# Two graph layers in one kernel: the second layer's loads issued by the sync engine, and its first 21 tiles gathered before the first layer's last rows are there

## The chip, the cores and the metric

One core of a Trainium2 chip runs the whole program. The metric is device microseconds of one execution; lower is better. The engines are named as the profile names them: PE is TensorE, DVE is VectorE, ACT is ScalarE, POOL is GpSimd, SP is SyncE. SP and ACT can issue plain DMA transfers; POOL issues the indirect ones, which gather or scatter 128 rows by a list of row numbers. Each engine works through its own instructions in the order in which the program lists them.

## The reference, cut to what matters

There are 6250 nodes with 256 features and 106250 edges, sorted by their destination. The last 6250 source rows belong to self loops. Both layers read one row per edge and sum over the edges that end in one node.

```python
x = _layernorm(x + L0(x, src, dst, edge_type_2))     # layer one
x = _layernorm(x + L1(x, [src, dst]))                # layer two

# L0: two relu products per edge, with the weights of the edge's type, summed by dst,
#     then gates, sigmoid, tanh and three small products per node
msgs = where(rel == r, relu(relu(S @ W.T + b) @ W.T + b), msgs)     # S = feat[src]
agg  = segment_sum(msgs, dst)

# L1: graph attention with 4 heads of 64
h     = x @ W
e     = leaky_relu(a_src[src] + a_dst[dst], 0.2)
ex    = exp(e - segment_max(e, dst)[dst])
out   = segment_sum(h[src] * ex / segment_sum(ex, dst)[dst], dst)
y     = relu(layernorm(out + x))
```

Layer two can read a node's row of `h` only after layer one has made that node.

## The kernel before

Edges other than the self loops are held as 782 tiles of 128 edges (TC). Seven tiles make a window of at most 64 destination nodes, 112 windows in all (NW), and two windows make a group of up to 128 nodes, 56 groups (NG). Self loops are handled with the node itself.

Before the layers, `gnn_kernel` reads the edge list, packs it, and turns it into lists by tile: the row numbers that layer one (`idx0`) and layer two (`idx1`) gather, each window's first node (`low_b`, a copy on every partition, and `low_i`), and the place of each edge's node in its window. In the same stretch, PE makes a table of messages, two rows a node (L1191, L1205, added up by DVE at L1213 and stored by SP at L1218); the code ties pieces of the list work to the blocks of this table, by hand.

`fast` then runs both layers under an order written out by hand: what each engine does is listed step by step, one step a tile. `Steps` holds chains of work as generators; `yield n` in a chain means "go on n steps later". `ring` hands out buffers in rotation, and a buffer's next use waits for its last reader.

Layer one: each step issues one gather on POOL (L1327) into one of ten buffers G of seven tiles each. LAG = 4 steps later PE multiplies the tile with a one-hot matrix of its nodes (`sum0`, L1689), which sums by node. After a group's last tile its rows go through `turn` and `update`: gates, products, normalization, and at L1625 the row of `h` with the logits a_src and a_dst behind it. ACT copies it into a buffer `hr` (L1629), and SP stores it into the DRAM table `rows1`, 64 rows a window (L1636). Windows overlap, so a store of 64 rows writes rows that the next store writes again. The last group's rows are scattered by POOL (L1638), since they end irregularly. Groups go through `update` in fours, then in twos, and the last four singly. The product that is kept for a node's own use later goes to the DRAM table `kept` (L1645).

Layer two: each step issues one gather of 128 rows of 260 numbers from `rows1` (L2002, through L1327) into the same ring of ten G. All of them come after all stores into `rows1`. LAG steps behind, when a window is complete, ACT copies its logits out of G (L2024; the first tile of the next group at L2016). Groups are taken in pairs, the last four singly (26 pairs and 4 groups):

- `ahead` loads what a pair needs from DRAM: the edges' places `dB` (L1764, four loads a pair) and the starts of the nodes' runs `cut` (L1771, two loads). Five steps later DVE turns dB into one-hot matrices (L1778), and PE fetches the nodes' logits with them (L1782).
- `weights` finds the largest logit of each node by scans and takes the exponential (L1822 to L1853).
- `weighted` multiplies a window's gathered rows by these weights: ACT copies the weights (L1873), DVE multiplies (L1874). This is the last reader of G.
- `sum1` sums by node on PE (L1983) and, at a group's first tile, loads `kept` rows into k3 (L1973).
- `finish` divides, normalizes twice on DVE and ACT (L1889 to L1935), and SP stores the result (L1940, two stores a group, again overlapping); POOL scatters the last group (L1942).

The loads at L1764, L1771 and L1973 are issued by ACT, in their place among ACT's copies and activations.

Of the kernel before, what the change touches and what calls it, by code (L numbers as in the profile page):

```python
# [33 lines left out]
F32 = mybir.dt.float32  # L34
I32 = mybir.dt.int32
# [39 lines left out]
NC = -(-EC // CT)  # L75
HA = D + H
LAG = 4
SORTED = "the fast path runs only where the chip has found the edges sorted"


# [623 lines left out]
def gnn_kernel(  # L704
# [37 lines left out]
    rows1 = dram.tile([NP + P, HA], F32, name="rows1")  # L742
    slots = dram.tile([NW, (WT + 1) * P], BF16, name="slots")
    cuts = dram.tile([(NC + 1) * CT, P], F32, name="cuts")
    kept = dram.tile([NG, P, 3 * D], F32, name="kept")
    packed = dram.tile([2 * BLOCKS, HB], I32, name="packed")

# [19 lines left out]
    mark = const.tile([P, COLS], BF16, name="fmark")  # L767
    tail_i = const.tile([P, 1], I32, name="tail_i")
    tail_x = const.tile([P, 1], I32, name="tail_x")


    with (
# [18 lines left out]
        with (  # L791
# [287 lines left out]
            late, turns = [], 0  # L1079
            src0 = src1  # L1080
            nc.vector.tensor_scalar(src0[:CT], src1[:CT], 1.0, None, op0=OP.subtract)
            for to, of in (
                (idx0, row),
                (dstE, list_f[:, :, 1:]),
                (mark, rel_f[:, :, :P]),
                (idx1, src0),
                (first, steps),
            ):
                for k0, kn in blocks_of(NC, 4):
                    pt = lps.tile([P, 4 * CT], F32, name="turned")  # L1090
# [15 lines left out]
                    for a, b, c in ((0, 1, 0), (1, 2, WT), (2, WT + 1, 1), (WT + 1, 2 * WT, WT + 1)):  # L1106
                        nc.vector.tensor_copy(to2[:, :, a:b], of2[:, :, c : c + b - a])
# [48 lines left out]

            nc.vector.tensor_scalar(tail_i, tail[:, 0:1], float(NP + P - 1), None, op0=OP.min)
            nc.vector.tensor_scalar(tail_x, tail[:, 0:1], float(NP - 1), None, op0=OP.min)


            for w0, wn in blocks_of(NW, P // (WT + 1)):
# [82 lines left out]
    with tc.If(odd_v == 0) as cmp:  # L1244
        fast(
            tc, x, WihT, bih, bhh, W1T, b1, W2T, b2, W3T, b3, Wg, att_src, att_dst, bias, gamma,
            beta, out, parts0, rows1, slots, cuts, kept, iota_f, iota_p, ident, idx0, idx1,
            first, mark, slot, low_i, tail_i, tail_x,
        )
    with cmp.Else():  # L1250
        general(
# [6 lines left out]
def fast(  # L1258
# [32 lines left out]
    low_i,  # L1291
    tail_i,
    tail_x,
):

    nc = tc.nc
# [27 lines left out]
        )[1]  # L1324

    def gather(to_tile, table, idx):
        nc.gpsimd.indirect_dma_start(  # L1327
            out=to_tile,
            out_offset=None,
            in_=table,  # L1330
            in_offset=bass.IndirectOffsetOnAxis(ap=idx, axis=0),
        )
# [46 lines left out]
    node3 = keep.tile([P, NG, 2, 3, 2 * H], BF16, name="node3")  # L1379
    nc.vector.memset(node3, 0.0)  # L1380
    loop = keep.tile([P, NG, H], F32, name="loop")
    vec = keep.tile([P, 2, D], F32, name="fvec")
    eps_c = keep.tile([P, 1], F32, name="eps_c")
    nc.vector.memset(eps_c, EPS)
# [32 lines left out]
    def in_order(done, g):  # L1417
        if g != len(done):
            raise ValueError("groups are out of order")
        done.append(g)  # L1420


    with (
# [32 lines left out]
        for k, v in enumerate((gamma, beta)):  # L1456
# [2 lines left out]
        nc.sync.dma_start(  # L1459
            rows1[N:, :].rearrange("(p r) f -> p (r f)", r=2),  # L1460
            zero[: (NP + P - N) // 2, : 2 * HA],
        )

        run = Steps()
# [24 lines left out]
        def turn(g, i, ps, aT):  # L1489

            agg = ring(up, [P, D], F32, "agg", 3)

            kind = ring(up, [P, 2], F32, "kind", 3)
            for r in range(2):
                nc.vector.tensor_scalar(  # L1495
                    kind[:, r : r + 1], ps[:, D:], float(3 - r), None, op0=OP.is_equal
                )
            for r, of in ((0, ps[:, :D]), (1, agg)):
                nc.vector.scalar_tensor_tensor(
                    agg,  # L1500
                    loop0[g][:, r * D : (r + 1) * D],
                    kind[:, r : r + 1],
                    of,
                    op0=OP.mult,
                    op1=OP.add,
                )
# [6 lines left out]
            nc.vector.tensor_copy(  # L1513
                aT[:, :, i * P : (i + 1) * P], pt.rearrange("p (k n) -> p k n", k=2)
            )

        def update(groups, aT):
            slow = min(3, max(1, (NG - 4 - groups[0]) // 4))
# [102 lines left out]
            for i, g in enumerate(groups):  # L1621
                u = everyone
                ph = ring(upp, [P, 4 * P], F32, "fpg", 5)[:, : D + 2 * H]
                for k in range(2):
                    nc.tensor.matmul(  # L1625
                        ph[u, :], hs[i][:, k, u], Wx[:, k, :], start=(k == 0), stop=(k == 1)
                    )
                hr = ring(up, [P, D + 2 * H], F32, "hr", 4)
                nc.scalar.copy(hr[u, :], ph[u, :])  # L1629
                nc.scalar.copy(keep3[i][u, 2, :], ph[u, :D])  # L1630

# [1 line left out]
                for w in windows_of(g):  # L1633
                    if w in at_w:
                        to = rows1[bass.ds(at_w[w], SLOTS), :]
                        nc.sync.dma_start(to, hr[half_of(w), :HA])  # L1636
                if g == NG - 1:
                    nc.gpsimd.indirect_dma_start(  # L1638
                        out=rows1,
                        out_offset=bass.IndirectOffsetOnAxis(ap=tail_i, axis=0),  # L1640
                        in_=hr[:, :HA],
                        in_offset=None,
                    )
                yield 1
                nc.sync.dma_start(kept[g, u, :], keep3[i][u, :, :].rearrange("p c f -> p (c f)"))  # L1645

# [53 lines left out]
        for n in range(TC + LAG):  # L1700
            if n < TC:
                g, t = order[n]
                k, turns = n % WT, n // WT // 10 % 2
                if k == 0:
                    seven = ring(rowsp, [P, WT * HA], F32, "G", 10).rearrange(
                        "p (j f) -> p j f", f=HA
                    )
                    m = min(WT, TC - n)
                    of, to = mark[:, n : n + m, None], seven[:, :, D : D + 1]
                    nc.scalar.copy(to[:, ::-1, :][:, :m, :] if turns else to[:, :m, :], of)  # L1710

                got[t] = seven[:, WT - 1 - k if turns else k, : D + 1]
                gather(got[t][:, :D], parts0, idx0[:, t : t + 1])
                if t == order_of(g)[0]:
                    ohs[g] = ring(ep, [P, 2 * W8, SLOTS], F32, "oh0", 2)
                    one_hot(ohs[g], 2 * g, 2 * W8)
                    loop0[g] = ring(up, [P, 2 * D], F32, "loop0", 2)
                    own_rows(g, lows_of(windows_of(g)), loop0[g], loops)
                    if g == NG - 1:
                        rows_x[g] = ring(up, [P, D], F32, "fxn", 8)  # L1720
                        own_rows(g, {}, rows_x[g], x)
            if n >= LAG:
                g, t = order[n - LAG]
                if t != 2 * WT * g:
# [4 lines left out]
                    sum0(g, 2 * WT * g)  # L1729
            run.step()  # L1730
        run.finish()


    with (
# [10 lines left out]

        nc.scalar.preload_act_table_set("natural_log_exp_and_others")
        run = Steps()
        G, late = {}, []

        def tiles_in(g):  # L1750

# [3 lines left out]
        def ahead(pair, box):  # L1755
# [5 lines left out]
            for g in pair:  # L1761
                dB = ring(ep, [P, W8, P], BF16, "dB", 3)
                for w in windows_of(g):
                    nc.scalar.dma_start(  # L1764
                        dB[half_of(w), :, :].rearrange("p j e -> p (j e)"),
                        at(slots, w * W8 * P, [[0, SLOTS], [1, W8 * P]]),
                    )
                dBs.append(dB)
            for i, g in enumerate(pair):
                n = len(tiles_in(g)[1])  # L1770
                nc.scalar.dma_start(  # L1771
                    cut[i * GS * H : (i * GS + n) * H, :],
                    at(cuts, tiles_in(g)[0][0] * P, [[P, n], [0, H], [1, P + 1]]),
                )
            yield 5
            for i, (g, dB) in enumerate(zip(pair, dBs)):
                ohT = ring(ep, [P, W8, P], BF16, "ohT", 2)
                nc.vector.tensor_scalar(ohT, dB, slot_p, None, op0=OP.is_equal)  # L1778
# [176 lines left out]
        def sum1():  # L1955
# [12 lines left out]
            if g not in sums:  # L1968
# [125 lines left out]
```

## Time and profile before

| | us |
|---|---|
| median of three runs | 2264.95 (2263.04 to 2268.02) |
| the profiled execution: its own time | 2266.64 |
| the profiled execution: span from first to last instruction | 2264.7 |
| first gather of layer one, last gather of layer one | 194.9, 1181.5 |
| first gather of layer two, last gather of layer two | 1213.8, 2198.2 |
| scatter of the last group's output | 2252.5 |

The page counts busy time by engine, and a row of an engine's timeline gives start, duration, engine, line, operation, what is written from what, and in brackets the idle time of the engine before it and what ended that. "issue" there means that no wait can be seen. ACTq, SPq and POOLq are the sequencers of these engines: a DMA's issue is not counted as busy time, but the engine does nothing else meanwhile. The granted TensorE clock has a mean of 0.81 in this execution.

### The profile page before, as it was taken

To read this page: it belongs to the slowest core of one execution; us is meant where nothing else is said; L and a number is where in the kernel's file an instruction comes from. 1 tells how busy PE (TensorE), PEld (TensorE's weight loads), DVE (VectorE), ACT (ScalarE), POOL (GpSimd) and SP (SyncE) were. 2 spreads that over 40 slices of the span, in tenths; PEclk is the share of its full clock that TensorE was granted. 3 is DMA by queue.
4 is the path that set the end of the run, shared out by engine and by line. 5 is a ranking of instruction groups with operands and counts; after the bars stand their busy time and mean duration, and the time that the engine had idled before them with its cause. 6 is when DMAs were issued, how large, how long until landed. Compare 5 with 4: busy or idle time off the path is not lost. (4 is left out here: it accounts for less than half of the span.)

```text
span 2264.7 us, 22022 instructions
## 1 busy us (share of the span) xinstructions
PE 1556.6 (69%) x5722; PEld 776.5 (34%) x5722; DVE 1237.3 (55%) x3333; ACT 508.5 (22%) x1526; POOL 1525.5 (67%) x1603
## 2 busy tenths in 40 slices
PE   8996788888888888988992355554545545454563
PEld 5663233333333333333551222222323223232331
DVE  7552133333343333433541667777776877777785
ACT  3331012222122221222342112111111111211211
POOL 1304777777777777777764777777777777777760
PEclk9998788989999989898996676766767677676776
DMA  5335445554555554555553555555555555555540
GB/s 163 131 99 157 128 128 156 168 165 143 151 155 170 165 151 143 155 170 165 176 155 91 138 161 145 154 147 155 152 149 161 144 156 151 148 156 150 156 137 27
DMA packets 163409, 332.53 MB, mean 147 GB/s; under 512 B 42467, under 2 KB 74306, under 8 KB 163273
## 3 DMA queue, kind: packets, MB, share of 16 engines
q0 software_dynamic: 75968, 208.00, 33.9%
q1 hardware_dynamic: 64736, 82.92, 11.4%
q10 hardware_dynamic: 22569, 40.12, 5.9%
q8 instruction: 47, 0.77, 0.2%
q14 instruction: 89, 0.73, 0.1%
HBM read 278.79 MB, written 52.12 MB: 146 GB/s over the span
## 5 line engine op out<-in xcount | busy, mean ns | idle before, releaser
L1327 POOL DMA_INDIRECT G<-parts,fidx x782 | 747.1, 955 | 327.5 <-issue 219.0
L1327 POOL DMA_INDIRECT G<-rows,fidx x782 | 747.5, 956 | 240.5 <-issue 222.9
L1689 PE MATMUL fps<-G,oh 128*64 128x257 f32 (+1 forms) x1674 | 533.1, 433 | 137.1 <-DMA G<-parts,fidx 120.6
L1983 PE MATMUL fps<-gw,oh 128*64 128x264 f32 (+1 forms) x1674 | 433.0, 469 | 238.3 <-DVE gw L1874 238.3
L1983 PEld LDWEIGHTS fps<-gw,oh 128*64 128x64 f32 (+1 forms) x1674 | 229.1, 168 | 412.8 <-DVE gw L1874 254.8
L1689 PEld LDWEIGHTS fps<-G,oh 128*64 128x64 f32 (+1 forms) x1674 | 196.6, 151 | 445.5 <-DMA G<-parts,fidx 226.7
L1874 DVE TENSOR_TENSOR gw<-G,bank 128x1792 f32<-128x1792 f32 (+1 forms) x167 | 249.0, 1491 | 175.0 <-ACT gw L1873 173.5
L1495 DVE TENSOR_SCALAR kind<-fps 128x1 f32<-128x1 f32 x112 | 12.5, 153 | 311.1 <-PE fps L1689 311.1
L1542 PE MATMUL fpg<-faT,fWihT 128*128 128x512 f32 (+2 forms) x432 | 171.6, 521 | 0.2 <-DVE faT L1513 0.2
L1822 PE MATMUL turn<-fident,e 128*120 128x128 f32 (+2 forms) x30 | 13.5, 449 | 219.4 <-ACT e L2016 219.4
L1410 DVE TENSOR_TENSOR oh<-bank,fslot 128x1024 f32<-128x1024 f32 x112 | 136.0, 1214 | 2.2 <-ACT bank L1853 2.2
L1923 ACT ACTIVATE frs<-fmv,eps_c 128x1 f32<-128x1 f32 x112 | 33.0, 294 | 306.0 <-DVE fmv L1922 152.0
L1650 DVE COPY nd<-hr 128x4 f32<-128x4 f32 x56 | 10.8, 193 | 160.1 <-ACT hr L1629 160.1
L1205 PE MATMUL fpm<-fWrT,fhT 128*128 128x256 f32 x392 | 91.7, 388 | 5.1 <-DVE fms L1213 5.1
L1542 PEld LDWEIGHTS fpg<-faT,fWihT 128*128 128x128 f32 x432 | 71.2, 191 | 68.9 <-issue 59.3
L1191 PE MATMUL fph<-fxc,fWrT 128*128 128x512 f32 (+1 forms) x208 | 88.9, 580 | 4.7 <-DMA fWrT<-in_WrT_dram 4.7
L1929 ACT ACTIVATE fy<-fy,frs 128x256 f32<-128x256 f32 x112 | 67.2, 600 | 98.4 <-DVE gw L1868 52.9
L1822 PEld LDWEIGHTS turn<-fident,e 128*120 128x120 f32 (+2 forms) x30 | 5.0, 166 | 233.2 <-ACT e L2016 231.6
L1205 PEld LDWEIGHTS fpm<-fWrT,fhT 128*128 128x128 f32 x392 | 74.9, 194 | 23.8 <-DVE fms L1213 8.8
L1873 ACT COPY gw<-bank 128x28 f32<-128x28 f32 (+1 forms) x167 | 28.5, 171 | 227.6 <-DMA dB<-slots 103.6
L1625 PE MATMUL fpg<-Wx,fyT 128*128 128x264 f32 x224 | 77.0, 474 | 3.0 <-ACT fyT L1616 3.0
L937 POOL DMA_INDIRECT packed<-frame,place x21 | 20.9, 995 | 77.6 <-DVE frame L902 71.5
(237 smaller groups left out, 1791.3 us busy)
## 6 DMA issues: line engine op xcount, KB each, us to landing
kept<-keep SPq DMA_DIRECT2D x56, 384.0 KB
k<-kept ACTq DMA_DIRECT2D x56, 384.0 KB
dB<-slots ACTq DMA_DIRECT2D x112, 128.0 KB
loop<-parts SPq DMA_DIRECT2D x110, 128.0 KB
parts<-fms SPq DMA_DIRECT2D x49, 256.0 KB
G<-parts,fidx POOLq DMA_INDIRECT x782
G<-rows,fidx POOLq DMA_INDIRECT x782
rows<-hr SPq DMA_DIRECT2D x110, 65.0 KB
```

The costliest lines, as they stand in the source:

```text
L1191: nc.tensor.matmul(ph[:, :cols], WrT_s[:, r, k, m * P : (m + 1) * P], xc[:, k, :cols], start=(k == 0), stop=(k == 1),)
L1205: made = nc.tensor.matmul(pm[:, r, :], hT[:, r, k, j * P : (j + 1) * P], WrT_s[:, r, k, :], start=(k == 0), stop=(k == 1),)
L1327: nc.gpsimd.indirect_dma_start(out=to_tile, out_offset=None, in_=table, in_offset=bass.IndirectOffsetOnAxis(ap=idx, axis=0),)
L1410: nc.vector.tensor_tensor(to[:, :nj, :], iota_s[:, None, :].to_broadcast([P, nj, SLOTS]), of[:, :, None].to_broadcast([P, nj, SLOTS]), op= ...
L1542: nc.tensor.matmul(pg[:, :cols], WihT_s[:, k, c * P : (c + 1) * P], aT[:, k, :cols], start=(k == 0), stop=(k == 1),)
L1625: nc.tensor.matmul(ph[u, :], hs[i][:, k, u], Wx[:, k, :], start=(k == 0), stop=(k == 1))
L1689: nc.tensor.matmul(sums[g][to, :], ohj, got[t], start=begins, stop=ends)
L1873: nc.scalar.copy(gw[:, :, D:HA], ex[:, o : o + n, :])
L1874: nc.vector.tensor_mul(gw[:, :, :D].rearrange("p j (h f) -> p j h f", h=H), of[:, :n, :D].rearrange("p j (h f) -> p j h f", h=H), ex[:, o ...
L1923: nc.scalar.activation(r, mv[u, k, 1:2], AF.Ln, bias=eps_c[u])
L1929: nc.scalar.activation(y, y, AF.Identity, bias=m, scale=r)
L1983: nc.tensor.matmul(sums[g][to, :], ohj, gw, start=begins, stop=ends)
```

## The change

Three things change.

1. The loads at L1764, L1771 and L1973 are issued by SP instead of ACT, and the reading of dB follows eight steps after them instead of five.
2. The first 21 tiles of layer two (EARLY, three windows) are gathered before layer one is done. 18 of these gathers are listed right behind layer one's last gather. They wait only for the rows of group 52 (NG - LATE - 1), by a wait that is added by hand, while the waits for the three later groups (LATE) are taken off. Three more gathers are listed behind the scatter of group 55, with a memset of one number in front. For them the row numbers `idx_e` name a row of zeros (NOROW) where the node belongs to one of the last three groups; they are made in the list stretch with some small DVE operations, as is `own_n`, the node number of each row of these three groups. The rows of `rows1` that those groups write are filled with zeros first, by one more transfer on SP.
3. What these tiles lack is added: the last three groups' rows stay in SBUF (`rows_l`, in place of a buffer `hr`, of which there are three instead of four). The edges' source numbers of the 21 tiles go to DRAM (`srcs`) and are read back on all partitions (three loads on ACT). For each of the three windows DVE compares them with `own_n`, three times 896 numbers, which gives one-hot matrices; for each tile PE multiplies three of these with `rows_l`, and DVE adds the product to the tile in G (`complete`).

```diff
+            behind.append((NB - 4, nc.sync.dma_start(srcs, src0[:EARLY, 0, :])))
...
+            for half, first_w, next_w in ((lo, w0, w0 + 1), (hi, w0 + 1, w0 + 2)):
...
+            before = lp.tile([P, EARLY], F32, name="before")
+            nc.vector.tensor_scalar(
+                before, idx1[:, :EARLY], low_b[:, w0 : w0 + 1], None, op0=OP.is_lt
+            )
...
+            nc.vector.tensor_scalar(idx_e, early_f, float(NOROW), None, op0=OP.add)
...
+        nc.sync.dma_start(
+            rows1[for_late:N, :].rearrange("(p r) f -> p (r f)", r=4),
+            zero[: (N - for_late) // 4, : 4 * HA],
+        )
...
+        def gather_early(n):
+            for t in range(len(early), n):
+                w = t // WT
+                if t % WT == 0:
+                    G[w] = ring(rowsp, [P, WT * HA], F32, "G", 10).rearrange(
+                        "p (j f) -> p j f", f=HA
+                    )
+                e = gather(G[w][:, t - WT * w, :], rows1, idx_e[:, t : t + 1])
+                for store in rest:
+                    tc.declare_no_dep(e.ins, store.ins, reason="rows of other nodes")
+                for store in whole:
+                    tc.add_manual_dep(
...
-                hr = ring(up, [P, D + 2 * H], F32, "hr", 4)
+                hr = ring(up, [P, D + 2 * H], F32, "hr", 3)
+                if g >= NG - LATE:
+                    hr = rows_l[:, g - (NG - LATE), :]
...
+            if n == TC:
+                gather_early(EARLY - 3)
...
+        nc.gpsimd.memset(pause, 0.0)
+        gather_early(EARLY)
...
+            nc.scalar.dma_start(srcb[w], at(srcs, w * WT * P, [[0, P], [1, WT * P]]))
+
+        def complete(t):
...
+                for q in range(LATE):
+                    nc.vector.tensor_scalar(
+                        srcb[w][1][:, q, :], srcb[w][0], own_n[:, q : q + 1], None, op0=OP.is_equal
+                    )
...
+            for q in range(LATE):
+                nc.tensor.matmul(
+                    more,
+                    srcb[w][1][:, q, j * P : (j + 1) * P],
+                    rows_l[:, q, :HA],
+                    start=(q == 0),
+                    stop=(q == LATE - 1),
+                )
+            nc.vector.tensor_add(G[w][:, j, :], G[w][:, j, :], more)
...
-                    nc.scalar.dma_start(
+                    nc.sync.dma_start(
                         dB[half_of(w), :, :].rearrange("p j e -> p (j e)"),
...
-                nc.scalar.dma_start(
+                nc.sync.dma_start(
                     cut[i * GS * H : (i * GS + n) * H, :],
...
-            yield 5
+            yield 8
...
-                nc.scalar.dma_start(k3s[g][u, :, :].rearrange("p c f -> p (c f)"), kept[g, u, :])
+                nc.sync.dma_start(k3s[g][u, :, :].rearrange("p c f -> p (c f)"), kept[g, u, :])
...
-            if t < TC:
+            if EARLY <= t < TC:
...
+                if k < EARLY:
+                    complete(k)
```

More of the change, by code (lines that the diff above doesn't have):

```diff
@@ L77 @@
 LAG = 4
+EARLY = 3 * WT
+LATE = 3
+NOROW = NP + SLOTS - 1
 SORTED = "the fast path runs only where the chip has found the edges sorted"
@@ L744, in gnn_kernel @@
     cuts = dram.tile([(NC + 1) * CT, P], F32, name="cuts")
+    srcs = dram.tile([EARLY, P], F32, name="srcs")
     kept = dram.tile([NG, P, 3 * D], F32, name="kept")
@@ L769, in gnn_kernel @@
     tail_x = const.tile([P, 1], I32, name="tail_x")
+    idx_e = const.tile([P, EARLY], I32, name="idx_e")
+    own_n = const.tile([P, LATE], F32, name="own_n")
     with (
@@ L1158, in gnn_kernel @@
             nc.vector.tensor_scalar(tail_x, tail[:, 0:1], float(NP - 1), None, op0=OP.min)
+            w0 = NW - 2 * LATE
+            held = lp.tile([P, LATE], F32, name="held")
+            for half, first_w, next_w in ((lo, w0, w0 + 1), (hi, w0 + 1, w0 + 2)):
+                o, v = own_n[half], held[half]
+                nc.vector.tensor_scalar(
+                    o,
+                    low_b[half, first_w : first_w + 2 * LATE - 1 : 2],
+                    iota_p[half],
+                    float(half.start or 0),
+                    op0=OP.add,
+                    op1=OP.subtract,
+                )
+                nc.vector.tensor_tensor(
+                    v, o, low_b[half, next_w : next_w + 2 * LATE - 1 : 2], op=OP.is_lt
+                )
+                nc.vector.scalar_tensor_tensor(o, o, 1.0, v, op0=OP.add, op1=OP.mult)
+                nc.vector.tensor_scalar(o, o, 1.0, None, op0=OP.subtract)
+            before = lp.tile([P, EARLY], F32, name="before")
+            nc.vector.tensor_scalar(
+                before, idx1[:, :EARLY], low_b[:, w0 : w0 + 1], None, op0=OP.is_lt
+            )
+            early_f = lp.tile([P, EARLY], F32, name="early_f")
+            nc.vector.scalar_tensor_tensor(
+                early_f, idx1[:, :EARLY], float(-NOROW), before, op0=OP.add, op1=OP.mult
+            )
+            nc.vector.tensor_scalar(idx_e, early_f, float(NOROW), None, op0=OP.add)
             for w0, wn in blocks_of(NW, P // (WT + 1)):
@@ L1247, in gnn_kernel @@
             beta, out, parts0, rows1, slots, cuts, kept, iota_f, iota_p, ident, idx0, idx1,
-            first, mark, slot, low_i, tail_i, tail_x,
+            first, mark, slot, low_i, tail_i, tail_x, idx_e, own_n, srcs,
         )
@@ L1293, in fast @@
     tail_x,
+    idx_e,
+    own_n,
+    srcs,
 ):
@@ L1326, in gather @@
     def gather(to_tile, table, idx):
-        nc.gpsimd.indirect_dma_start(
+        return nc.gpsimd.indirect_dma_start(
             out=to_tile,
@@ L1381, in fast @@
     loop = keep.tile([P, NG, H], F32, name="loop")
+    rows_l = keep.tile([P, LATE, D + 2 * H], F32, name="rows_l")
     vec = keep.tile([P, 2, D], F32, name="fvec")
@@ L1420, in in_order @@
         done.append(g)
+    G = {}
     with (
@@ L1461, in fast @@
             zero[: (NP + P - N) // 2, : 2 * HA],
+        )
+        for_late = N - 2 * LATE * SLOTS
+        nc.sync.dma_start(
+            rows1[for_late:N, :].rearrange("(p r) f -> p (r f)", r=4),
+            zero[: (N - for_late) // 4, : 4 * HA],
         )
@@ L1515, in turn, with keep_row @@
             )
+        whole, rest, early = [], [], []
+        pause = keep.tile([P, 1], F32, name="pause")
+        def keep_row(g, store):
+            if g == NG - LATE - 1:
+                whole.append(store)
+            if g >= NG - LATE:
+                rest.append(store)
+                last = store.ins.engine == mybir.EngineType.Pool
+                for e in early[: len(early) - last]:
+                    tc.declare_no_dep(store.ins, e.ins, reason="rows of other nodes")
+        def gather_early(n):
[4 more added lines that the diff above has]
+                        "p (j f) -> p j f", f=HA
+                    )
+                e = gather(G[w][:, t - WT * w, :], rows1, idx_e[:, t : t + 1])
[3 more added lines that the diff above has]
+                    tc.add_manual_dep(
+                        e.ins,
+                        store.ins.name,
+                        mybir.DependencyInfo(
+                            mybir.DependencyClass.Sync, mybir.DependencyReason.DATA
+                        ),
+                        reason="the rows that were stored by then",
+                    )
+                early.append(e)
         def update(groups, aT):
@@ L1627, in update @@
                     )
-                hr = ring(up, [P, D + 2 * H], F32, "hr", 4)
+                hr = ring(up, [P, D + 2 * H], F32, "hr", 3)
+                if g >= NG - LATE:
+                    hr = rows_l[:, g - (NG - LATE), :]
                 nc.scalar.copy(hr[u, :], ph[u, :])
@@ L1635, in update @@
                         to = rows1[bass.ds(at_w[w], SLOTS), :]
-                        nc.sync.dma_start(to, hr[half_of(w), :HA])
+                        keep_row(g, nc.sync.dma_start(to, hr[half_of(w), :HA]))
                 if g == NG - 1:
-                    nc.gpsimd.indirect_dma_start(
+                    move = nc.gpsimd.indirect_dma_start(
                         out=rows1,
@@ L1643, in update @@
                     )
+                    keep_row(g, move)
                 yield 1
@@ L1747, in fast @@
         run = Steps()
-        G, late = {}, []
+        late = []
+        srcb = []
+        for w in range(EARLY // WT):
+            srcb.append(ring(ep, [P, WT * P], F32, "srcb", 3))
+            nc.scalar.dma_start(srcb[w], at(srcs, w * WT * P, [[0, P], [1, WT * P]]))
+        def complete(t):
+            w, j = t // WT, t % WT
+            if j == 0:
+                srcb[w] = (srcb[w], ring(ep, [P, LATE, WT * P], F32, "ohS", 1))
+                for q in range(LATE):
+                    nc.vector.tensor_scalar(
+                        srcb[w][1][:, q, :], srcb[w][0], own_n[:, q : q + 1], None, op0=OP.is_equal
+                    )
+            more = ring(eps, [P, D + 2 * H], F32, "fps1", 2)[:, :HA]
+            for q in range(LATE):
[5 more added lines that the diff above has]
+                    stop=(q == LATE - 1),
+                )
+            nc.vector.tensor_add(G[w][:, j, :], G[w][:, j, :], more)
         def tiles_in(g):
```

## The prediction

> **What bounds the kernel now.** I read the page first, then GpSimd's timeline round the change of layers and at the end, the waits inside layer two, and one steady pair of groups on ScalarE and VectorE. Busy time by engine on the page:
>
> ```profile
> PE 1556.6 (69%) x5722; PEld 776.5 (34%) x5722; DVE 1237.3 (55%) x3333; ACT 508.5 (22%) x1526; POOL 1525.5 (67%) x1603
> ```
>
> POOL's 67% is 1564 gathers of 0.95 us, one after the other. Its timeline round the change of layers and at the end (start, duration, engine, line, idle before and what ended it):
>
> ```profile
> 1181.46 0.94 POOL L1327 DMA_INDIRECT G<-parts,fidx  x1 [0.30 <-issue]
> 1210.18 1.00 POOL L1638 DMA_INDIRECT rows<-hr,tail_i  x1 [27.77 <-ACT keep L1630]
> 1213.78 0.96 POOL L1327 DMA_INDIRECT G<-rows,fidx  x1 [2.60 <-issue]
> 1215.05 0.95 POOL L1327 DMA_INDIRECT G<-rows,fidx  x1 [0.31 <-issue]
> ...
> 2198.24 0.95 POOL L1327 DMA_INDIRECT G<-rows,fidx  x1 [0.30 <-issue]
> 2252.49 1.01 POOL L1942 DMA_INDIRECT out_dram<-fy,tail_i  x1 [53.30 <-POOLq L1244]
> ```
>
> A gather takes a slot of 1.25 us (0.95 and 0.30 of issue). Between the layers POOL stands still for 27.8 us until group 55 has its rows, then 2.6 us more until they have landed. After the last gather 53.3 us pass before the last store.
>
> That suggests that layer two is bound by gathers. It isn't: the copies of the gathered logits on ScalarE (L2024) show how far the other engines are behind.
>
> ```profile
> 1224.47 0.21 ACT L2024 COPY e<-G 128x28 f32<-128x28 f32 x1 [11.02 <-DMA G<-rows,fidx]
> ...
> 2223.85 0.19 ACT L2024 COPY e<-G 128x20 f32<-128x20 f32 x1
> ```
>
> The first window's copy comes 2.0 us after its last gather ended (1222.4) and waited for it. The last one's comes 24.7 us after 2199.2 and waited for nothing. The lag grows in every pair of groups: 35.83 us a pair for the arithmetic (the multiplications that free windows 4 and 100 end at 1302.9 and 2162.9, 24 pairs apart), 35.29 us for the gathers (1249.0 and 2095.9). So layer two is now bound by VectorE and what it waits for, by half a microsecond a pair; the ring of ten G buffers hides it from POOL. Stretch of 24 pairs, busy by engine (PE, PEld, DVE, ACT, POOL), then the waits of layer two (total, times, longest):
>
> ```profile
> 1302.90:2162.90 860.00, 430.99 (x1970) 242.63 (x1969) 641.86 (x1634) 165.05 (x673) 651.91 (x684) 0.69 0.56 152
> ```
> ```profile
> DVE gw L1874 <- ACT gw L1873: 171.2, 143, 5.2
> ACT gw L1873 <- DMA dB<-slots: 103.6, 25, 4.5
> ```
>
> VectorE is busy 641.86 / 24 = 26.7 us a pair and idle 9.1, of which 171.2 / 25 = 6.8 stands behind a ScalarE copy. Why that copy is late, in one pair:
>
> ```profile
> 1784.15 2.45 ACTq L1764 DMA_DIRECT2D dB<-slots  x4
> 1786.64 1.82 ACTq L1771 DMA_DIRECT2D cut<-cuts  x2
> 1788.51 0.16 ACT L1873 COPY gw<-bank 128x4 f32<-128x4 f32 x1 [4.22 <-DMA dB<-slots]
> ```
> ```profile
> 1783.64 0.13 DVE L1868 TENSOR_TENSOR gw<-topE,ffirst 128x4 f32<-128x4 f32 x1
> 1788.70 0.42 DVE L1874 TENSOR_TENSOR gw<-G,bank 128x256 f32<-128x256 f32 x1 [4.93 <-ACT gw L1873]
> ```
>
> ScalarE issues six loads, 4.3 us, in front of a copy of 0.16 us, and VectorE stands idle 4.93 us for it, once a pair.
>
> **What the Trainium skill says.** "DMA: Bandwidth & Descriptors", section "Issuing engines are not separate DMA queues": all issuers share the same 16 DMA engines, so another issuer saves only sequencer time. The trace agrees that it is sequencer time that hurts (4.3 us above); the bytes stay. The same page, "Anatomy of one DMA", gives about 2.0 us plus bytes / 436 GB/s; the 2.6 us behind the move at 1210.18 agree. "VectorE: DVE Perf Modes", "The perf-mode tier table": fp32 tensor_scalar from SBUF at twice the rate of tensor_tensor; here 126x896 took 0.61 us (L1081) against 1.07 (L1059).
>
> **The change, part by part.**
>
> *Early gathers.* The first needs group 52's rows: stored at 1163.50 and 1166.08, so landed long before 1182.4 by the 2.6 us above. 18 gathers from 1182.7 end by 1205.2 in POOL's idle stretch; hidden wholly. The move stays at 1210.18: it now waits also for the 18th gather's landing (1204.9 + 2.6 = 1207.5, earlier). Behind it the memset (unseen here; 0.1 to 0.3 us) and three gathers to about 1215.2: the landing of the move, 1213.8, passes below them. Tile 21 is gathered from 1215.5 instead of 1240.25: **-24.75 us** on POOL, with all 761 others behind it.
>
> *Completing 21 tiles.* ScalarE issues three broadcasts of 458 KB after its table load, at 1213.4; by the page's formula 3 us each (an estimate), so the first is there at about 1218, others a few us on, more if they share with gathers and slot loads. VectorE: 9 one-hots x 0.61 = 5.5 us, 21 additions x 0.42 (as L1909) = 8.8: 14.3 us. TensorE: 63 fp32 products with 128 weight columns and 260 wide. The profile shows each as two instructions (L1205: 49 x 4 calls, x392):
>
> ```profile
> 183.18 7.07 PE L1205 MATMUL fpm<-fWrT,fhT 128*128 128x256 f32 x32
> ...
> 1207.36 2.13 PE L1625 MATMUL fpg<-Wx,fyT 128*128 128x264 f32 x4 [0.46 <-ACT fyT L1616]
> ```
>
> So 7.07 / 16 = 0.44 us at a warm clock and 2.13 / 2 = 1.06 at its worst; 63 cost 28 to 67 us. Work is dense, so I take 30: tile 20 complete at about 1250. Pair 0 starts its weights at 1252.1 now (tile 28 has landed) and then at about 1250.5: -1.5, bounds -8 and +13 (a cold array for half of it). Those microseconds delay no gather as long as the G ring holds: G[0] is free at 1265.6 now, so 1264; POOL wants it for tile 70 at 1215.5 + 49 x 1.25 = 1276.8. Margin 13 us, cost 0; at the upper bound 2 us.
>
> *Loads to SyncE.* 112 dB, 56 cut and 56 k loads leave ScalarE. The pair loses the 4.93 us: 30.9 instead of 35.83. They now queue behind the output stores of the same queue, the second of which waits for the first one's landing:
>
> ```profile
> SPq L1940 <- DMA out_dram<-fy: 196.9, 109, 4.5
> ```
>
> That is 1.8 us a store. In the pair above the two stores go at 1777.93 and 1781.36, so SP is free at 1782 and could issue dB at 1783, when ScalarE did; reading comes 8 steps later instead of 5. SP's own work: four stores of about 2.5 us and six loads, 5 us: 15 of 31. So cost 0; the work hiding it is those 8 steps (about 10 us), of which landing wants some 3. The pair is then bound by the gathers at 35.29 and wins back 4.4 us a pair: the 23 us that the arithmetic is behind POOL at the start are gone after six of 26 pairs.
>
> *The end.* Caught up, lag is 2 us where it is 11.1 at window 104 now. The last four groups are made singly: their arithmetic takes 2150.7 to 2223.85 = 73.1 us for 59.5 us of gathers; less 2 for loads not issued by ScalarE, the lag grows by 11.6 to 13.6, not 24.7: **-11.1** (bounds 0, and -22.7 if it doesn't grow). What follows the last L2024, 41 us, stays.
>
> *Layer one and before.* About eleven VectorE operations of 0.15 to 0.25 us near 149 to 162, where table making waits for VectorE: 0 to +2.5, taken **+1**. One more store in front of the last tables (0.5 us; the last waits for ScalarE at 1191.70 anyway) and the zero fill on SP (0.5 us; the loop0 rows behind it are wanted at 216): 0. hr from four buffers to three: copies of a quad lie at 613.5, 618.8, 625.9 and 630.7, so the first is stored 11 us before its reuse: 0; bound +2.
>
> Sum: -24.75 + 0.2 - 11.1 + 1 = -34.7. Against the profiled execution's 2266.64 (span 2264.7): 2232; against the median of 2264.95, whose runs lie between 2263.04 and 2268.02: 2230. I say **2231**.
>
> **Rivals.** (a) *The pair stays slow in part*: loads land late, or another wait opens where ScalarE's was. With period p the arithmetic alone ends 1.5 + 26 x (35.83 - p) earlier; the whole gain needs p below 34.5, and at 35.1 it is 20 us: 2238 to 2258. For it: 9.1 us idle a pair have other parts too. Against: 4.93 is one wait with one cause. (b) *The early gathers do not run early*, because a wait for layer one's last rows remains: POOL as now, the lag still closes: -11 + 1 = 2255. (c) *Nothing*: p stays 35.8, 2263. (d) *Slower*: SP serves dB late. Reading has 7.7 us now and three steps (3.8) more; with 3 to land, 8.5 us of lateness are free, each one above costs 26 us over the layer, and from 13.4 on the 4.9 saved are lost; 14 us late is p = 36.4, 26 x 0.6 - 1.5 = +14: 2279. It would need an output store to land in some 17 us, not 3.4.
>
> **How the numbers follow.** Likeliest 0.64 (own range 2224 to 2238), better than that 0.04, (a) 0.14, (b) 0.08, (c) 0.05, (d) 0.05. Range 2223 to 2250: it leaves out (c), (d) and the weaker ends of (a) and (b). A change under 0.2% (4.5 us) can't be told from none: faster 0.90, same 0.05, slower 0.05.
>
> **What would show it.** 18 gathers of rows between 1182 and 1206, the first late tile near 1215, the last gather near 2174; VectorE's wait for L1873's ScalarE copy near 2 us a pair and a lag of L2024 near 2 us in mid-layer. Wrong if POOL waits for G buffers, if the completing matmuls end after 1264, or if ohT waits for dB in every pair.

## The result and the profile after

The changed kernel takes 2230.81 us (median of four, 2225.75 to 2232.09) where the kernel before takes 2265.33 (median of four, 2263.04 to 2268.02): ratio 0.984, 95% interval 0.9822 to 0.9858. The profiled execution took 2231.32 us, its span is 2229.5. The chips of experiments 1 to 3 and of experiment 6 are of this kind (the kernel before takes 2265.81 and 2269.18 us there), but the changed kernel itself was not timed on them. On the two chips of experiment 5 the kernel before needs 3066 and 3050 us, and there the changed kernel is slower by 0.6 to 0.7%.

Busy time by engine, from the page of the changed kernel:

```profile
PE 1576.9 (71%) x5848; PEld 789.2 (35%) x5848; DVE 1259.0 (56%) x3374; ACT 506.4 (23%) x1526; POOL 1527.2 (68%) x1604
```

DVE, PE and PEld did a little more than before (21.7, 20.3 and 12.7 us, the completing), ACT and POOL the same within 2.1 us. The gain is idle time. GpSimd's timeline of the changed kernel, round the change of layers and at the end:

```profile
1184.73 0.95 POOL L1367 DMA_INDIRECT G<-parts,fidx  x1 [0.30 <-issue]
1185.98 0.95 POOL L1367 DMA_INDIRECT G<-rows,idx_e  x1 [0.30 <-DMA G<-parts,fidx]
...
1207.69 0.95 POOL L1367 DMA_INDIRECT G<-rows,idx_e  x1 [0.30 <-issue]
1213.99 1.00 POOL L1725 DMA_INDIRECT rows<-rows_l,tail_i  x1 [5.35 <-ACT keep L1717]
...
1219.07 0.95 POOL L1367 DMA_INDIRECT G<-rows,fidx  x1 [0.30 <-issue]
...
2177.11 0.95 POOL L1367 DMA_INDIRECT G<-rows,fidx  x1 [0.30 <-issue]
2217.15 1.00 POOL L2060 DMA_INDIRECT out_dram<-fy,tail_i  x1 [39.10 <-ACT fy L2047]
```

The 18 early gathers stand directly behind layer one's last; 5.35 us of the old hole of 27.77 are left; tile 21, the first that isn't early, comes 5.1 us after the scatter of group 55 (the prediction calls it the move), where it came 30.1 after it before. Behind the last gather 39.1 us are idle instead of 53.3. In between, no gather waits more than some 0.3 us. The copies of the gathered logits on ScalarE (first window, and last):

```profile
1234.31 0.21 ACT L2144 COPY e<-G 128x28 f32<-128x28 f32 x1 [17.05 <-DVE G L1866]
...
2188.92 0.19 ACT L2144 COPY e<-G 128x20 f32<-128x20 f32 x1
```

The first is now late, since it waits for the completing of its tiles. The last one comes 10.9 us after its window's gathers (2178.1), not 24.7. Below, "lag" is this time from the end of a window's last gather to the copy of its logits. One pair of groups, the timelines of ScalarE, of VectorE and of SyncE's sequencer:

```profile
1791.06 0.14 ACT L1991 COPY gw<-bank 128x4 f32<-128x4 f32 x1
```
```profile
1791.23 0.42 DVE L1992 TENSOR_TENSOR gw<-G,bank 128x256 f32<-128x256 f32 x1 [0.60 <-ACT gw L1991]
```
```profile
1788.84 2.41 SPq L1882 DMA_DIRECT2D dB<-slots  x4
1791.30 1.85 SPq L1889 DMA_DIRECT2D cut<-cuts  x2
```

The 0.14 us copy no longer stands behind six issues, and the multiplication waits 0.60 us for it, not 4.93. The waits of layer two (1260 to 2160; total, times, longest):

```profile
DVE gw L1992 <- ACT gw L1991: 59.6, 142, 0.7
```

Before, it was 171.2 us, longest 5.2.

The span is 35.2 us shorter, and the two traces give it in pieces (before, after, difference):

| piece | before | after | difference |
|---|---|---|---|
| start to the move of group 55 | 1210.18 | 1213.99 | +3.8 |
| move to tile 21 | 30.07 | 5.08 | -25.0 |
| tile 21 to the last gather | 957.99 | 958.04 | +0.1 |
| last gather to the last copy of logits | 25.61 | 11.81 | -13.8 |
| last copy of logits to the last scatter | 28.64 | 28.23 | -0.4 |
| last scatter to the end | 12.21 | 12.35 | +0.1 |

### The profile page after: what moved, and what is told of

Its sections match the earlier page's. It is cut to its first block, busy times and chain, and to the rows that moved or that the text cites. A ratio compares the mean times of both kernels' runs of the same rounds, so it can differ in the third digit from the quotient of the medians.

```text
span 2229.5 us, 22334 instructions
## 1 busy us (share of the span) xinstructions
PE 1576.9 (71%) x5848; PEld 789.2 (35%) x5848; DVE 1259.0 (56%) x3374; ACT 506.4 (23%) x1526; POOL 1527.2 (68%) x1604
## 5 line engine op out<-in xcount | busy, mean ns | idle before, releaser
L1367 POOL DMA_INDIRECT G<-rows,fidx x761 | 727.4, 956 | 231.8 <-issue 214.2
L2101 PEld LDWEIGHTS fps<-gw,oh 128*64 128x64 f32 (+1 forms) x1674 | 222.7, 164 | 411.9 <-DVE gw L1992 266.0
L1545 DVE TENSOR_SCALAR kind<-fps 128x1 f32<-128x1 f32 x112 | 12.5, 153 | 315.0 <-PE fps L1777 315.0
L1242 PE MATMUL fpm<-fWrT,fhT 128*128 128x256 f32 x392 | 92.9, 392 | 5.3 <-DVE fms L1250 5.3
L1627 PEld LDWEIGHTS fpg<-faT,fWihT 128*128 128x128 f32 x432 | 70.9, 190 | 69.1 <-issue 59.4
L1250 DVE TENSOR_TENSOR fms<-fpm,fbrr 128x512 f32<-128x512 f32 x49 | 33.6, 688 | 68.7 <-PE fpm L1242 62.8
L2144 ACT COPY e<-G 128x28 f32<-128x28 f32 x112 | 23.8, 213 | 183.8 <-DMA G<-rows,fidx 147.2
```

The lines of the kernel that those rows point to most:

```text
L1242: made = nc.tensor.matmul(pm[:, r, :], hT[:, r, k, j * P : (j + 1) * P], WrT_s[:, r, k, :], start=(k == 0), stop=(k == 1),)
L1250: nc.vector.tensor_add(ms.rearrange("p r f -> p (r f)"), pm.rearrange("p r f -> p (r f)"), brr)
L1367: return nc.gpsimd.indirect_dma_start(out=to_tile, out_offset=None, in_=table, in_offset=bass.IndirectOffsetOnAxis(ap=idx, axis=0),)
L1627: nc.tensor.matmul(pg[:, :cols], WihT_s[:, k, c * P : (c + 1) * P], aT[:, k, :cols], start=(k == 0), stop=(k == 1),)
L2101: nc.tensor.matmul(sums[g][to, :], ohj, gw, start=begins, stop=ends)
```

## The experiments

The theory: the early gathers win 25 us on GpSimd, the loads on SyncE let the arithmetic follow GpSimd, completing the tiles is hidden by the ring of ten G buffers, and each part needs the other. The rivals: one part does it all; completing is on the path; the loads cost nothing where they were.

**1. The loads alone.** The kernel before, with only the three load sites and the number of steps changed:

```diff
-                    nc.scalar.dma_start(
+                    nc.sync.dma_start(
...
-                nc.scalar.dma_start(
+                nc.sync.dma_start(
...
-            yield 5
+            yield 8
...
-                nc.scalar.dma_start(k3s[g][u, :, :].rearrange("p c f -> p (c f)"), kept[g, u, :])
+                nc.sync.dma_start(k3s[g][u, :, :].rearrange("p c f -> p (c f)"), kept[g, u, :])
```

> The kernel before, with only the loads of dB, cut and kept rows moved to SyncE and dB read eight steps later. Theory (in layer two the arithmetic was the bound by half a microsecond a pair, because ScalarE's issues stand in front of its copies; without them the gathers bind at 35.3 us a pair): gathers end where they did, near 2199; the last logit copy lags about 11 us behind the last gather instead of 24.7; the wait of VectorE for the weight copy falls from 171 to some 60 us; the time is 2265 - 14 = 2251. Rival (gathers alone bind layer two, ScalarE's issues cost nothing): 2265, lag still 24.7. Rival (loads come late behind the output stores): waits of the one-hot step for dB in most pairs, 2265 or more.

Measured 2253.12 us (2251.73 to 2257.25) beside 2265.81 for the kernel before; ratio 0.9945, interval 0.9929 to 0.9962. From the timelines of GpSimd and ScalarE of this kernel:

```profile
2196.10 0.94 POOL L1327 DMA_INDIRECT G<-rows,fidx  x1 [0.30 <-issue]
```
```profile
2209.16 0.19 ACT L2024 COPY e<-G 128x20 f32<-128x20 f32 x1
```

The gathers end where they ended, within the spread between executions (the last one starts 2.1 us earlier than the 2198.24 before); the last copy follows 12.1 us behind its gathers instead of 24.7. So these issues did cost time, nearly all of it in the lag at the end: in mid-layer GpSimd bounds, with a lag of 2 to 4 us. VectorE's wait for the copy of the weights fell from 171.2 to 59.4 us. The later reading of dB was not tried apart from the new issuer; in the kernel before VectorE has no wait for dB in layer two that the later reading could have removed. The theory held.

**2. The early gathers alone.** The changed kernel, with the same three sites back on ScalarE and `yield 5`.

> The changed kernel with the loads of dB, cut and kept rows back on ScalarE, five steps ahead: the early gathers alone. Theory (arithmetic binds at 35.8 us a pair, and a lead of the gathers is then worth nothing): the first pair's weights start some 5 us later than before, since 63 products stand in front; the lead ends as POOL waiting for a G buffer or as lag; the time is 2265 + 2 for the list + 5 = 2271 (2265 to 2276). Rival (the 24 us of POOL's idle time are on the path whatever the loads do): 2241.

Measured 2265.48 us (2260.34 to 2267.82), ratio 0.9991, interval 0.9983 to 1.0. Timelines of GpSimd and ScalarE, then a line of the waits of layer two (1260 to 2160), of this kernel:

```profile
2174.77 1.00 POOL L1367 DMA_INDIRECT G<-rows,fidx  x1 [0.30 <-issue]
2248.12 1.01 POOL L2060 DMA_INDIRECT out_dram<-fy,tail_i  x1 [72.35 <-ACT fy L2047]
```
```profile
2219.51 0.19 ACT L2144 COPY e<-G 128x20 f32<-128x20 f32 x1
```
```profile
DVE gw L1992 <- ACT gw L1991: 165.9, 140, 5.2
```

The gathers end even earlier than in the changed kernel, and the time is that of the kernel before: GpSimd then stands idle for 72.35 us. VectorE waits 165.9 us for the copy as it did before, a pair takes 35.8 us, and the 24 us of lead become lag: 43.7 us at the last window. The rival of 2241 fell. The 2271 of the theory was some 5 us too high. Completing did put off the first pair, as it said: the first G buffer comes free 59.8 us after the move (1267.35 from 1207.58), in the kernel before 55.4 (1265.56 from 1210.18). But that was made up by window 4, which is released 92.9 us after the move here (1300.5) and 92.7 in the kernel before (1302.9).

Together with experiment 1: the parts alone bring 12.7 and about 0 us, both bring 34.5 (in the result above). The early gathers shorten what only bounds once the loads are moved.

**3. Without completing, and with twice the products.** In the first, the edges of the last three groups are left out in the 21 tiles; in the second every product is made twice (the second sum replaces the first, so that the values stay).

```diff
-                if k < EARLY:
-                    complete(k)
```
```diff
-            for q in range(LATE):
+            for q in [*range(LATE), *range(LATE)]:
```

> The changed kernel without completing the 21 tiles: no one-hots, no products, no additions, so the edges from the last three groups are missing in these tiles. Theory (the 31 us of products lie beside gathers, and the G ring holds): the first logit copy comes 10 to 25 us earlier, the lag of 23 us at the start is gone earlier, but the gathers stand where they stood and the end with them: 2231, within 3. Rival (the products are on the path): 2231 - 31 = 2200.

> The changed kernel with each of the 63 products made twice (the second sum replaces the first, so the values stay). Theory (the cover is the G ring: 11.9 us of margin between the release of the first G buffer and the gather of tile 70): the products last about 62 us, the first G buffer is released near 1301, POOL waits for it once, about 20 us near 1281, and every later gather is 20 us later: 2251 (2245 to 2256). Rival (there is no such limit, arithmetic catches up all the same): 2231.

Without completing: 2226.34 us (2225.07 to 2228.07), ratio 0.9822, interval 0.9805 to 0.9838, which overlaps that of the changed kernel. The expectation of 2231, within 3, is missed by 1.7 us; the changed kernel was not timed on this chip, so the times alone leave room for a cost of a few us. The traces show none on GpSimd's path: here tile 21 comes 5.06 us after the move and the last copy 10.9 us after its gathers, as in the changed kernel; and of the 4.9 us between the two profiled executions, 4.0 lie ahead of the move, where both kernels do the same. The first G buffer is free at 1243.4 instead of 1269.2, and that brings nothing: the margin of the ring, from there to the gather of tile 70, which is the first to use that buffer again, goes from 11.9 to 33.2 us, and tile 21 to the last gather takes 957.0 us where it took 958.0. The 11.9 us are read from these two lines of the changed kernel, VectorE's multiplication that frees the buffer and GpSimd's gather of tile 70:

```profile
1267.16 2.02 DVE L1992 TENSOR_TENSOR gw<-G,bank 128x1792 f32<-128x1792 f32 x1 [0.15 <-ACT gw L1991]
```
```profile
1281.06 0.95 POOL L1367 DMA_INDIRECT G<-rows,fidx  x1 [0.30 <-issue]
```

With twice the products: 2249.69 us (2245.52 to 2250.38), ratio 0.9925, interval 0.9909 to 0.9942. GpSimd's timeline of this kernel at tile 70:

```profile
1295.26 0.95 POOL L1367 DMA_INDIRECT G<-rows,fidx  x1 [17.81 <-DVE gw L1992]
```

The first G buffer comes free at 1295.0, and GpSimd waits 17.81 us for it, once. That is 83.7 us after the move (1211.27), where it was 55.2 in the changed kernel: of 28.5 us more, 11 were covered, and the rest came through whole (18.9 us between the two medians). The expectation was met. So the cover is the ring of G, and its size is the margin read at tile 70.

**4. What the list operations cost.** The kernels of experiments 2 and 3 have the eleven VectorE operations that make `idx_e` and `own_n` and the kernel of experiment 1 has not, so their traces answer this too. Layer one's first gather starts, without the operations, at 194.91 (the kernel before), 194.51 and, in experiment 6, 195.11; with them at 196.91 (the changed kernel), 193.91, 194.48 and 194.60. The means are 194.84 and 194.98: no cost is to be seen beside a spread of 3 us. Nor did layer one start earlier on the chips of experiment 5 with these operations moved out of its way: 208.1 to 209.3 with the list later, 206.1 to 208.0 without.

**5. More early tiles, and the list later.** GpSimd's 5.35 idle us ahead of the move have room for four more gathers, so three kernels were made of the changed one: 25 early tiles (22 ahead of the move; four broadcasts of the source numbers instead of three), the list operations moved into layer one, and both. On a first chip all three ran beside the changed kernel, on a second one the two with 25 early tiles.

```diff
-EARLY = 3 * WT
+EARLY = 3 * WT + 4
```

> The changed kernel once more, as the yardstick of the next three: 2231 us (2226 to 2234), every theory.

> The changed kernel, with the eleven VectorE operations that make idx_e and own_n moved out of the list stretch into layer one. Theory (these operations delay table making and so layer one's first gather by 2 to 3 us; nothing in layer one waits for VectorE there): first gather of layer one near 194.5 instead of 196.9, time 2228 (2226.5 to 2229.5). Rival (the late first gather is spread between runs, not these operations): 2231.

> The changed kernel with 25 early tiles instead of 21 (22 gathers ahead of the move, 3 behind it). POOL is idle for 5.35 us ahead of the move, which is room for four more gathers of 1.25; four more tiles to complete cost four times 1.31 us, hidden by the ring of G while its margin of 11.9 us stays above zero: 11.9 - 5.0 - 5.3 = 1.6. Theory: last gather of layer two 5 us earlier, time 2226 (2224 to 2228.5), no wait of POOL for a G buffer. Rival (completing is on the path: the products set when layer two starts): 2231 to 2233.

> Both of the last two edits. Theory: they add, since one shifts everything from layer one on and the other shifts layer two alone: 2223 (2221 to 2226). Rival: the margin of G is used up and the second edit gives nothing on top of the first: 2228.

> The changed kernel as the yardstick of the next two, in a job of its own since the chip of the last job needed 3066 us for the kernel before, not 2265. Every theory, where the kernel before needs 2265: 2231 us (2226 to 2234). Where it needs about 3066 again: 3082.

> The changed kernel with 25 early tiles instead of 21 (22 gathers ahead of the move, 3 behind it). POOL is idle for 5.35 us ahead of the move, which is room for four more gathers of 1.25; four more tiles to complete cost four times 1.31 us, hidden by the ring of G while its margin of 11.9 us stays above zero: 11.9 - 5.0 - 5.3 = 1.6. Theory: last gather of layer two 5 us earlier, no wait of POOL for a G buffer, 5 us less than the yardstick of this job (4 to 6.5; 2226). Rival (completing is on the path: the products set when layer two starts): no less than the yardstick, up to 2 us more.

> 25 early tiles, and also the eleven VectorE operations that make idx_e and own_n moved out of the list stretch into layer one. Theory (these operations delay table making and so layer one's first gather by 2.8 us, and nothing in layer one waits for VectorE there): first gather of layer one near 194 instead of 196.9, and 2 to 3 us less than with 25 early tiles alone (2223, 2221 to 2226). Rival (the late first gather of the changed kernel comes from the spread of executions, not from these operations): the same as with 25 early tiles alone.

| | first chip, us | ratio to the kernel before, interval | second chip, us | ratio, interval |
|---|---|---|---|---|
| kernel before | 3065.92 | 1 | 3049.96 | 1 |
| changed kernel | 3082.23 | 1.0058 (1.0036 to 1.008) | 3076.02 | 1.0073 (1.0041 to 1.0104) |
| list later | 3077.22 | 1.004 (1.0022 to 1.0059) | | |
| 25 early | 3089.67 | 1.0077 (1.0047 to 1.0108) | 3077.28 | 1.008 (1.0052 to 1.0107) |
| 25 early, list later | 3081.81 | 1.0058 (1.0037 to 1.0079) | 3082.63 | 1.0103 (1.0065 to 1.0141) |

Every expectation that was put for a kernel before of 2265 us failed. What was put for a slower chip came closer: 3082 for the changed kernel (3076.02 on the second), and of 25 early tiles there the rival's no gain (1.3 us more than the changed kernel). The intervals are too wide for 3 or 5 us, and whether 25 early tiles are better where the kernel before takes 2265 us stays open. What these traces do show is a second regime, in which the forecast is wrong. Of the 859 us that the span of the changed kernel is longer on the second chip, layer one's gathers take 242 (1230.2 us from first to last against 987.8) and those of layer two from tile 21 on 532 (1489.8 against 958.0). GpSimd's timeline of the changed kernel on the second of these chips, then VectorE's, with the additions of `complete` and in brackets the wait ahead of each:

```profile
1570.73 0.95 POOL L1367 DMA_INDIRECT G<-rows,fidx  x1 [0.30 <-issue]
1619.57 0.95 POOL L1367 DMA_INDIRECT G<-rows,fidx  x1 [47.90 <-DVE gw L1992]
```
```profile
1529.95 0.42 DVE L1866 TENSOR_TENSOR G<-G,fps 128x260 f32<-128x260 f32 x1 [11.11 <-remote]
1546.05 0.43 DVE L1866 TENSOR_TENSOR G<-G,fps 128x260 f32<-128x260 f32 x1 [15.68 <-remote]
...
1578.02 0.42 DVE L1866 TENSOR_TENSOR G<-G,fps 128x260 f32<-128x260 f32 x1 [14.88 <-remote]
1588.21 0.43 DVE L1866 TENSOR_TENSOR G<-G,fps 128x260 f32<-128x260 f32 x1 [0.29 <-PE fps L1859]
```

While GpSimd gathers, four additions wait 11 to 16 us, though the matmuls of a product take 1.3 to 3 us; some microseconds after GpSimd has stopped at 1571.7, the next waits fall to 0.3 to 2.4. In layer two the same falls on the scans of nearly every pair (VectorE, then GpSimd's last gather of the stretch and the next one):

```profile
1986.63 0.42 DVE L1947 TENSOR_TENSOR_SCAN s<-cut,turn 120x128 f32<-120x128 f32 x1 [22.35 <-remote]
```
```profile
1980.36 0.95 POOL L1367 DMA_INDIRECT G<-rows,fidx  x1 [0.30 <-issue]
2001.08 0.95 POOL L1367 DMA_INDIRECT G<-rows,fidx  x1 [19.77 <-DVE gw L1992]
```

In 24 of the 26 pairs the first scan waits 22 to 23 us (538.1 in sum), and each time it starts 4.5 to 6.0 us after GpSimd's gathers have stopped. "remote" means that the profile names no releaser: the scan reads `turn`, which PE writes, and `cut`, which a DMA loads, and which of the two comes late isn't shown. Not every hand-over is late: under the same gathers VectorE's waits for a named ScalarE or PE instruction stay at or below 1.9 us from 1510 to 3030, and PE starts a product 0.06 us after the addition that it waits for (1530.43 after 1530.37). Nor is it the work: a gather takes what it took (median 0.949 us against 0.946), and PE is busy 1556.1 us where it was 1576.9, though its granted clock has a mean of 0.723 instead of 0.829. GpSimd fills the ring, stops for its buffers, and only then do these waits end: its waits for G sum to 523.0 us in 25 stops, the first of 47.9 and the others of 19.8 in the mean. What the change puts under the gathers loses its cover in this trace: the move comes 66.5 us after layer one's last gather (1438.97 to 1505.46; 28.3 in the trace of the result, 1185.68 to 1213.99), and the products for 21 tiles take 93 us (1513.3 to 1606.4) instead of 35. With 25 early tiles, on the same chip, GpSimd's first stop is 52.5 us instead of 47.9: the lead of four more gathers, 5 us, is handed back in the first wait.

**6. The loads alone once more.** The kernel of experiment 1 was to tell which part loses in that regime.

> The kernel before with the loads on SyncE alone, once more, since on the chips of the last two jobs the changed kernel lost to the kernel before (3082 against 3066 us, 3076 against 3050) and a signal from one engine to another took 11 to 16 us there while GpSimd gathered. If this job's chip is such a one. Theory (the loads still gain there, and the early part loses: the last groups of layer one are made under gathers, so that the move of group 55 comes 66 us after layer one's last gather and not 29, and completing 21 tiles takes over 100 us, so the first G buffers come free at about 1615): the move 30 to 40 us after the last gather of layer one, the first G buffer free near 1520 to 1540, pairs of 54.6 us as in the changed kernel, time 2980 to 3010, ratio 0.98. Rival (the loads behind SyncE's output stores are what loses there): 3080 or more, over the kernel before. If the chip is as the first one: 2253 again (2250 to 2257), ratio 0.9945.

The chip was one of the quicker kind: 2255.81 us (2253.38 to 2259.42) beside 2269.18, ratio 0.9945, interval 0.9928 to 0.9961. It repeats experiment 1 and leaves the question open: which of the two parts loses on the slower chips, and why waits end late there, isn't settled. The two stretches above are where the changed kernel's trace points; there is no trace of the kernel before on such a chip to compare.

## Why the prediction was right

It said 2231 us and the measurement is 2230.81; in the profiled execution it said -34.7 and the span shrank by 35.2. The mechanism is the one said: each part was needed, as experiments 1 and 2 show. The terms are less exact than the sum.

- **Early gathers**: -24.75 and +0.2 said; -25.0 measured from the move to tile 21. The 18 gathers ran from 1185.98 to 1208.6 (1182.7 to 1205.2 said; layer one ended 3.3 us later in this execution).
- **Completing**: hidden, as said, though it took longer. The first pair's scans start at 1258.1, 44.1 us after the move, where 40.3 was said (1250.5 from 1210.2). The start was right: the first one-hot stood at 7.8 us after the move in the prediction (1218 from 1210.2) and came at 7.3 (1221.30 from 1213.99). The 3 us for a broadcast came from a fit that is given for transfers issued by GpSimd, while these are ScalarE's; the first is used 4.8 us after its issue (1216.50). What was too small is the time from there to tile 20, 32 us said (1218 to 1250) and 35.8 measured (1221.30 to 1257.09): a window's three one-hots wait until the last window's products are done, since `ohS` has one buffer, so that products and one-hots hardly overlap. The product itself was sized right (1.31 us a tile, three times 0.44). The two lines from which the prediction took 0.44 and 1.06 us lie at granted clocks of 1.00 and 0.50; over these products it was 0.93. The margin of the ring was 11.9 us; 13 had been said.

VectorE's timeline at the beginning and at the end of completing, in the changed kernel:

```profile
1221.30 1.95 DVE L1853 TENSOR_SCALAR ohS<-srcb,own_n 128x896 f32<-128x896 f32 x3 [6.42 <-DMA dB<-slots]
1225.04 0.43 DVE L1866 TENSOR_TENSOR G<-G,fps 128x260 f32<-128x260 f32 x1 [1.79 <-PE fps L1859]
...
1256.66 0.43 DVE L1866 TENSOR_TENSOR G<-G,fps 128x260 f32<-128x260 f32 x1 [0.89 <-PE fps L1859]
1258.08 0.42 DVE L1947 TENSOR_TENSOR_SCAN s<-cut,turn 120x128 f32<-120x128 f32 x1 [1.00 <-PE turn L1940]
```

The bracket of the first line names dB, but the one-hots read the broadcast source numbers; a releaser is inferred.

- **The pair**: 30.9 us said where the arithmetic bounds, 32.3 measured (windows 4 to 24 are released at 1299.2 and 1460.7, five pairs). The stretches of five pairs, changed kernel and then kernel before, columns as in the prediction:

```profile
1299.20:1460.70 161.50, 88.20 (x411) 48.69 (x410) 134.19 (x342) 34.04 (x140) 122.51 (x129) 0.71 0.57 157
```
```profile
1302.90:1482.05 179.15, 88.90 (x408) 50.41 (x407) 132.15 (x341) 34.76 (x140) 135.88 (x143) 0.69 0.55 151
```

  A pair went from 35.83 to 32.30. VectorE's wait for the copy fell from 35.2 to 11.7 us in these stretches, 4.7 a pair; its busy time rose by 0.4, its waits for the ScalarE results `frs` and `bank` by 0.7 together. The term that was too large is the 4.93, taken as won whole: the work behind the wait moved up and met other waits. The miss cost nothing, as 32.3 is still under the gathers' 35.3; the lag of 22.9 us at window 4 was 3.9 at window 24 and 2.1 at window 32 (six pairs said).
- **The end**: -11.1 said, -13.8 measured. The lag grows from 3.1 at window 104 to 10.9 at the last, by 7.8 us and not 11.6: ScalarE's issues held up the four single groups by more than the 2 us that were taken off. The experiments bear that out: with the loads on SyncE the lag grows over the same windows by 8.6 and 7.7 us (experiments 1 and 6), with them on ScalarE by 12.5 and 13.6 (experiment 2 and the kernel before).
- **List and layer one**: +1 said, and no cost seen (experiment 4). The +3.8 us of this execution ahead of the move lie within the spread between executions; 2.8 more than said there and 2.7 less than said at the end are two misses that have nothing to do with each other and cancelled: that the sum came within 0.5 us is luck.
- **SyncE**: cost 0 said, and seen: the second output store's wait for the first fell from 196.9 to 102.9 us in sum, dB is issued at 1788.84 for a reading at 1798.28, and VectorE never waits for dB in mid-layer. Rival (d), loads late behind the stores, did not come about on this kind of chip. Rivals (a), (b) and (c) fell with the 32.3, the 1185.98 and the ratio.

What the prediction didn't see is that its numbers hold for one kind of chip: no step of it asked what happens to the cover if a wait under gathers ends 15 us late.

## What to carry to other kernels

Where one engine leads and the others follow with a lag that grows, a gain on the leading engine is worth nothing until the followers' period is below the leader's: measure both periods first, and make the follower's change first or with it. Here the work hidden by a ring of buffers showed no cost up to the margin at the first reuse and cost its full length beyond it, so the margin (11.9 us) is the number to read before more is hidden there.

## What the hardware showed beyond that

- The issue of a load costs SyncE what it costs ScalarE: 2.41 and 2.45 us for the four of dB, 1.85 and 1.82 for the two of cut. As the Trainium skill has it ("DMA: Bandwidth & Descriptors", "Issuing engines are not separate DMA queues"), another issuer saves only the sequencer's time; in experiment 1, where the same bytes were loaded by another issuer and read three steps later, that time was worth 12.7 us.
- On two chips the kernel before took 1.35 times as long (3065.92 against 2265.33) and the changed one 1.38 times (3082.23 against 2230.81). In the changed kernel's trace a gather and VectorE's largest multiplication take there what they take on the quicker chip (0.949 and 0.946 us, 2.021 and 2.021), but single waits of VectorE in layer two last 11 to 25 us and end under GpSimd's gathers or shortly after them.
- Between executions on the quicker chips, the start of layer one's gathers varied from 193.9 to 196.9 us and their length from 986.1 to 988.5: a difference of 3 us between two single profiles means nothing.
